# Reading each attention accumulator once, with two engines in turn, in a four-layer graph network

## The chip, the cores and the metric

The kernel runs on one core of one Trainium2 chip. The metric is the device time of one execution in microseconds (us), the median of several runs. All inputs lie in the chip's DRAM when it starts, and the result is written back there.

The core has a matrix engine (TensorE; in the profile PE for its matmuls and PEld for its weight loads), a vector engine (VectorE, DVE), a scalar engine for functions such as exp (ScalarE, ACT), a general engine (GpSimd, POOL) and an engine whose queue here only issues transfers (SyncE, SP). Each engine takes the instructions of its own queue in order; an instruction that waits holds up all that stand behind it on its engine. Matmul results go to PSUM[...]; all else lies in SBUF, 128 partitions wide.

## The reference

Four layers work on 4096 nodes with 256 features and one 4096 x 4096 adjacency matrix of zeros and ones. Each layer normalises its input, applies relu, runs a graph layer, and adds the result to the input:

```
h = max(layernorm(x), 0);  x = x + layer(h, adj)
layer 0: Wh = h @ W
         e  = leaky(Wh @ a_src + (Wh @ a_dst).T, 0.2), masked by adj
         h_attn = softmax(e, axis=1) @ Wh
         (then a dense part: several gated projections of Wh and h_attn)
layer 1: (adj == 1) @ h / degree @ W.T + b
layer 2: h2 = h @ W
         e  = leaky(h2 @ a[:256] + (h2 @ a[256:]).T, 0.01), masked by adj
         elu(softmax(e, axis=1) @ h2)
layer 3: softmax((h @ Wq) @ (h @ Wk).T, masked) @ (h @ Wv)
```

elu(z) is z where z is positive and exp(z) - 1 elsewhere. The change concerns the end of the attention in layers 0 and 2: the product of weights and values is divided by the sum of the weights, and in layer 2 elu is applied and the layer's input added.

## The kernel before

The state xs (128 x 32 x 256, float32) holds all 4096 rows in SBUF throughout, as 32 row tiles of 128 rows. Layers 0 and 2 share the class `Attention` (L160 to L314). It works on 8 blocks of four row tiles (RB = 4). For a block, the 4096 columns are gone through in 16 pairs of column tiles. The work on a pair is:

- `reach` (L216): DVE takes a running minimum over the mask codes of a later block (L229), which gives each row's largest logit. At the end of a block the minimum is transposed on TensorE (L238), reduced on DVE (L241 to L246), transposed back (L248), and sent through DRAM so that every partition has it as a row (L251, L253). `reach` runs 19 pairs ahead of the logits in the text of the program.
- `logits` (L258): DVE makes the logits y of four row tiles and one column tile (L265, twice a pair), POOL subtracts the mask code (L269). There are 8 buffers for y.
- three pairs later (`lag`), ACT takes the exponential (L295, twice a pair), and TensorE multiplies the four row tiles by the values v, which have 257 columns, the last of them ones (L306). The four products of a block gather in four PSUM accumulators `acc` of 128 x 257. Layer 0 has four such buffers, layer 2 five.
- after a block's last pair (L310 to L314), for each of its four row tiles: DVE takes the reciprocal of column 256 (L313), and `finish` is called.

`finish0` (L328 to L330) is one ACT instruction per row tile: acc times the reciprocal, into xs. `finish2` (L737 to L744) is four per row tile: ACT reads acc for exp (L740) and once more for relu (L742), then DVE adds min(exp, 1) and xs (L743), and relu and -1 (L744). The first product of the next block that needs an accumulator in use can start only when all reads of it are done.

In layer 0 the adjacency is read as it comes and transposed on TensorE (L348), turned into codes by ACT (L352) and stored; in layer 2 the codes come from DRAM (`stored`, L748 to L752) in pieces of 1 MB, four to a block, issued by SP (L751) into 7 buffers. A buffer is free again when POOL has subtracted the last pair of its piece.

The text of the program doesn't fix the order of the instructions on an engine. The framework that builds the program (Tile) lays them out by their dependencies and its own estimate of when each can run, and adds the waits; the order on the chip is then fixed. In the trace, running minima (L229) of later blocks stand between the steps of the block that ends.

PSUM, y and `turned` buffers are given out in the same way. Layer 3's preparation (L812 to L835) starts from xs right after layer 2, with its first tiles in the SBUF space that layer 2 leaves.

Of the kernel before, what the change touches and what calls it, by code (L numbers as in the profile page):

```python
# [11 lines left out]
F32 = mybir.dt.float32  # L12
# [3 lines left out]
AF = mybir.ActivationFunctionType  # L16
ALU = mybir.AluOpType
# [4 lines left out]
P = 128  # L22
# [19 lines left out]
def kernel(ctx: ExitStack, tc: tile.TileContext, w: dict, out: bass.AP):  # L42
    nc = tc.nc
    x, adj = w["x"], w["adj"]
    N, D = x.shape
# [8 lines left out]
    RB = 4  # L54
# [5 lines left out]
    const = ctx.enter_context(tc.tile_pool(name="const", bufs=1))  # L60
# [7 lines left out]
    ones = const.tile([P, P], F32, name="ones")  # L68
# [5 lines left out]
    xs = state.tile([P, NT, D], F32, name="xs")  # L74
# [49 lines left out]
    def preln(small, xb, h):  # L124

        mv = small.tile([P, BT, 2], F32, tag="pl_mv", name="pl_mv")
        for i in range(BT):
            stats_of(small, xb[:, i, :], mv[:, i, :], "pl")
        rs = rstd_of(small, mv, BT, "pl")
        off = small.tile([P, BT], F32, tag="pl_off", name="pl_off")  # L130
        nc.vector.scalar_tensor_tensor(off, mv[:, :, 0], -1.0, rs, ALU.mult, ALU.mult)
        for i in range(BT):
            nc.scalar.activation(
                h[:, i, :], xb[:, i, :], AF.Relu, scale=rs[:, i : i + 1], bias=off[:, i : i + 1]
            )
        return mv
# [23 lines left out]
    class Attention:  # L160
# [110 lines left out]
        def run(self, es, lead, n_acc, ahead=lambda n: None):  # L271

            self.y_p = es.enter_context(tc.tile_pool(name=f"{self.tag}_y", bufs=self.n_y))
            self.ps_b = es.enter_context(
                tc.tile_pool(name=f"{self.tag}_b", bufs=1, space=PSUM)
            )
            ps_acc = es.enter_context(
                tc.tile_pool(name=f"{self.tag}_acc", bufs=n_acc, space=PSUM)
            )
            pairs = [(b, c) for b in range(NRB) for c in range(0, NT, 2)]  # L280
            LAG = self.lag
            ys, accs = {}, {}
            for n in range(len(pairs) + LAG):
                if n < len(pairs):
                    b, c = pairs[n]
                    ahead(n)
                    if n + PPB + lead < len(pairs):
                        self.reach(n + PPB + lead)
                    ys[n] = y = self.y_p.tile([P, RB, 2, P], F32, tag="y", name="y")
                    self.logits(y, b, c, self.turned(b, c // QT))  # L290
                if n >= LAG:
                    b, c = pairs[n - LAG]
                    y = ys.pop(n - LAG)
                    for k in range(2):
                        nc.scalar.activation(  # L295
                            y[:, :, k, :], y[:, :, k, :], AF.Exp,
                            bias=self.sdst[:, c + k : c + k + 1],
                        )
                    if c == 0:
                        accs[b] = [  # L300
                            ps_acc.tile([P, D + 1], F32, tag="acc", name="acc")
                            for _ in range(RB)
                        ]
                    for k in range(2):
                        for r in range(RB):
                            nc.tensor.matmul(  # L306
                                out=accs[b][r], lhsT=y[:, r, k, :], rhs=self.v[:, c + k, :],
                                start=(c + k == 0), stop=(c + k == NT - 1),
                            )
                    if c == NT - 2:  # L310
                        for r, acc in enumerate(accs.pop(b)):
                            rden = self.small.tile([P, 1], F32, tag="rden", name="rden")
                            nc.vector.reciprocal(rden, acc[:, D : D + 1])  # L313
                            self.finish(b * RB + r, acc, rden)  # L314


    LEAD = 3
# [1 line left out]
    with ExitStack() as l0:  # L319
# [5 lines left out]
        bcw = w_early.tile([P, KD, 2 * S + 1], F32, name="bcw")  # L325
        bcb = w_early.tile([P, 2 * S + 1], F32, name="bcb")
        with ExitStack() as es:
            def finish0(t, acc, rden):  # L328

                nc.scalar.mul(xs[:, t, :], acc[:, 0:D], rden)  # L330

            turned = {}
            att = Attention(l0, es, "l0", 0.2, 3, 8, lambda b, q: turned[b, q], finish0)
# [23 lines left out]
            def ahead(n):  # L357
                if n + UPB + FRESH < NRB * UPB:
                    fresh(n + UPB + FRESH)
                if n % RB == 0:  # L360
                    b, q = n // UPB, n % UPB // RB
                    nc.sync.dma_start(out=codesT[b][q], in_=turned[b, q])
# [371 lines left out]
    with ExitStack() as es:  # L734
        work2 = es.enter_context(tc.tile_pool(name="l2_work", bufs=2))

        def finish2(t, acc, rden):  # L737

            e = work2.tile([P, D], F32, tag="e", name="e")
            nc.scalar.activation(e, acc[:, 0:D], AF.Exp, scale=rden)  # L740
            hp = work2.tile([P, D], F32, tag="hp", name="hp")
            nc.scalar.activation(hp, acc[:, 0:D], AF.Relu, scale=rden)  # L742
            nc.vector.scalar_tensor_tensor(e, e, 1.0, xs[:, t, :], ALU.min, ALU.add)  # L743
            nc.vector.scalar_tensor_tensor(xs[:, t, :], hp, -1.0, e, ALU.add, ALU.add)  # L744

        loaded = {}

        def stored(b, q):  # L748
            if (b, q) not in loaded:
                loaded[b, q] = turned_p.tile([P, RB, QT, P], BF16, tag="turned", name="turned")  # L750
                nc.sync.dma_start(out=loaded[b, q], in_=codesT[b][q])  # L751
            return loaded[b, q]  # L752

        att = Attention(es, es, "l2", 0.01, 3, 8, stored, finish2)
        turned_p = es.enter_context(tc.tile_pool(name="l2_turned", bufs=7))
        with ExitStack() as ps_:
            wp = ps_.enter_context(tc.tile_pool(name="l2_w", bufs=1))
            work = ps_.enter_context(tc.tile_pool(name="l2_prep", bufs=2))
            small = ps_.enter_context(tc.tile_pool(name="l2_s", bufs=4))
            pst = ps_.enter_context(tc.tile_pool(name="l2_pst", bufs=3, space=PSUM))  # L760
            psm = ps_.enter_context(tc.tile_pool(name="l2_psm", bufs=3, space=PSUM))
            att.weights(wp, work, w["L2_gnn_W"], (w["L2_gnn_a"],))

            def block2(b):
                h = work.tile([P, BT, D], F32, tag="h", name="h")
                preln(small, xs[:, ts(b, BT), :], h)
                yield
                hT = transposed_block(work, pst, h, "hT")
                yield
                att.project(b, hT, psm)  # L770
                yield
                for n in range(2 * b, 2 * b + 2 if b < NB - 1 else PPB + LEAD):
                    att.reach(n)

            run_staggered([block2(b) for b in range(NB)], 2)

        att.run(es, LEAD, 5)
# [233 lines left out]
```

## Time and profile before

| | |
|---|---|
| median of 3 runs | 3105.68 us (3105.03 to 3110.4) |
| profiled execution, its own time | 3108.19 us |
| span of its trace | 3106.4 us |
| TensorE matmul busy | 2881.5 us (93%) |
| DVE / ACT / POOL busy | 1847.5 / 1282.5 / 870.1 us |
| attention of layer 0 | about 111 to 632 us of the span |
| attention of layer 2 | about 1638 to 2135 us |
| granted TensorE clock, mean | 0.972 of full speed |

The table is read with the stages in mind: busy shares of the whole span mix stages with different limits. In the two attention stages TensorE does the same products, and what the other engines do shows only where TensorE stands still. A group of the profile's page has the line, engine, operation and tiles, the count, then the busy time and the mean length in ns, then the idle time of the engine just before these instructions and what ended most of it. A wait for several things is put down to the one that came last. Durations of the instructions concerned, from the trace (minimum / median / maximum in ns): L330 453/462/479, L740 452/473/498, L742 458/468/507, L743 415/420/1209, L744 415/420/2161, L313 141/168/170.

### The profile page before, as it was taken

Reading aid. Unit: us, or ns where it says so; the run is one execution under the profiler, and the core shown is the slowest. Engines: PE = TensorE matmul, PEld = TensorE weight load, DVE = VectorE, ACT = ScalarE, POOL = GpSimd, SP = SyncE. Lnnn points to the kernel's source line nnn. Section 1 sums busy time; section 2 is a strip of 40 time slices with the busy share of each in tenths; the row PEclk is TensorE's granted clock in tenths of the full one; section 3 lists DMA queues with packets and bytes.
Section 4 is the critical chain, followed back from the end, with each engine's and each line's share of the span. In section 5 each row is a group of like instructions: output and inputs, shape, how many; then the busy total and the mean of one; then the engine's idle time right before and its main releaser. Section 6 shows DMA issues by size and latency. Waiting matters only on the chain.

```text
span 3106.4 us, 34931 instructions
## 1 busy us (share of the span) xinstructions
PE 2881.5 (93%) x13344; PEld 2343.0 (75%) x13344; DVE 1847.5 (59%) x3322; ACT 1282.5 (41%) x1980; POOL 870.1 (28%) x604
## 2 busy tenths in 40 slices
PE   5799999979999999699968999899999999999999
PEld 4688888845555565588857887788888888888888
DVE  5767667324444444544479877755866656656653
ACT  5556655368888884400044443444111211211211
POOL 3556665533232332100016555562000000000000
PEclk9899999989999999899989999999999999999999
DMA  8666664054444441234222221202111111111100
GB/s 209 143 130 137 132 132 106 7 186 129 130 128 127 124 135 37 87 118 140 95 103 80 85 78 69 75 8 68 57 38 33 60 38 33 60 38 33 60 8 7
DMA packets 103128, 268.75 MB, mean 87 GB/s; under 512 B 10704, under 2 KB 24272, under 8 KB 94768
## 3 DMA queue, kind: packets, MB, share of 16 engines
q1 hardware_dynamic: 79104, 220.30, 21.3%
q0 software_dynamic: 22464, 45.51, 8.6%
q8 instruction: 104, 1.70, 0.2%
q10 hardware_dynamic: 1392, 0.72, 0.1%
q14 instruction: 64, 0.52, 0.1%
HBM read 262.22 MB, written 37.81 MB: 97 GB/s over the span
## 4 chain that ended last, share of the span: by engine, by line
PE 34%; issue 28%; ACT 11%; DMA 10%; DVE 10%; POOL 6%; POOLq 0%; ACTq 0%; SPq 0%; DVEq 0%
PE acc L306 16%; PE acc L717 8%; DMA a<-in_adj_dram 6%; PE mm L150 5%; ACT sign L507 5%; POOL y L269 4%; DVE run L229 3%; PE s L150 3%; DVE y L265 2%; PE acc L943 2%; DMA turned<-codesT 1%; DMA ab_row<-l_ab_d 1%; ACT zT L492 1%; ACT t L481 1%; ACT y L295 1%
## 5 line engine op out<-in xcount | busy, mean ns | idle before, releaser
L306 PE MATMUL acc<-v,y 128*128 128x257 f32 x4096 | 930.1, 386 | 52.9 <-ACT hp L742 27.8
L306 PEld LDWEIGHTS acc<-v,y 128*128 128x128 f32 x4096 | 777.2, 192 | 168.3 <-ACT hp L742 32.2
L269 POOL TENSOR_TENSOR y<-y,turned 128x1024 f32<-128x1024 f32 x256 | 544.0, 2137 | 323.1 <-DVE y L265 272.6
L295 ACT ACTIVATE y<-y,sdst 128x512 f32<-128x512 f32 x512 | 343.1, 715 | 359.7 <-POOL y L269 359.7
L265 DVE SCALAR_TENSOR_TENSOR y<-ab_row,cdst,b 128x512 f32<-128x512 f32 x512 | 361.4, 742 | 175.8 <-PE acc L306 110.1
L943 PE MATMUL acc<-v,y 128*128 128x257 f32 x2048 | 454.5, 380 | 0.4 <-DVE rden L951 0.4
L150 PE MATMUL s<-qT,hT 128*128 128x256 f32 x2048 | 445.2, 379 | 0.7 <-ACT qT L891 0.7
L150 PEld LDWEIGHTS s<-qT,hT 128*128 128x128 f32 x2048 | 389.0, 190 | 54.2 <-ACT qT L891 1.4
L943 PEld LDWEIGHTS acc<-v,y 128*128 128x128 f32 x2048 | 387.1, 190 | 55.9 <-issue 0.8
L936 ACT ACTIVATE y<-y 128x1024 f32<-128x1024 f32 x128 | 132.2, 1055 | 714.3 <-DVE y L935 710.0
L229 DVE SCALAR_TENSOR_TENSOR run<-turned,sd,run 128x512 f32<-128x512 bf16 x496 | 373.2, 752 | 68.1 <-DMA turned<-codesT 45.4
L507 ACT ACTIVATE sign<-a,limits 128x1024 bf16<-128x1024 int32 x256 | 294.0, 1148 | 85.4 <-DMA a<-in_adj_dram 81.2
L956 POOL DMA_DIRECT2D out_dram<-o x32 | 17.4, 542 | 934.9 <-DVE rden L951 932.0
L717 PE MATMUL acc<-v,eq 128*128 128x512 f32 x1024 | 240.3, 396 | 0.0
L905 DVE SCALAR_TENSOR_TENSOR y<-code,s 128x512 f32<-128x512 bf16 x256 | 175.8, 687 | 100.9 <-PE s L150 100.6
L717 PEld LDWEIGHTS acc<-v,eq 128*128 128x128 f32 x1024 | 191.9, 188 | 46.6 <-DVE eq L713 0.3
L935 DVE TENSOR_TENSOR y<-y,top 128x1024 f32<-128x1024 f32 x128 | 146.2, 1214 | 43.0 <-PE top L929 43.0
L912 DVE TENSOR_TENSOR mx<-mx,y 128x512 f32<-128x512 f32 x224 | 154.8, 691 | 7.5
L352 ACT ACTIVATE turned<-cT,log_wide 128x1024 bf16<-128x1024 bf16 x128 | 141.6, 1106 | 33.6 <-PE cT L348 33.3
L713 DVE TENSOR_SCALAR eq<-code 128x4096 fp32r<-128x4096 bf16 x32 | 73.4, 2294 | 115.8 <-PE acc L717 115.8
L150 PE MATMUL mm<-hsT,w_L_gnn_W_hz 128*128 128x512 f32 x256 | 118.3, 601 | 1.7 <-DVE hsT L570 1.7
L348 PE MATMUL cT<-identb,adj_t 128*128 128x128 bf16 x1024 | 83.2, 226 | 36.6 <-DVE identb L67 18.6
(219 smaller groups left out, 2742.8 us busy)
## 6 DMA issues: line engine op xcount, KB each, us to landing
a<-in_adj_dram SPq DMA_DIRECT2D x128, 512.0 KB, 3.7
adj_t<-in_adj_dram POOLq DMA_DIRECT2D x128, 256.0 KB, 4.5
codesT<-turned SPq DMA_DIRECT2D x32, 1024.0 KB, 5.2
code<-codesT SPq DMA_DIRECT2D x128, 256.0 KB, 3.8
turned<-codesT SPq DMA_DIRECT2D x32, 1024.0 KB, 4.9
code<-codesT SPq DMA_DIRECT2D x64, 512.0 KB, 4.8
ab_row<-l_ab_d SPq DMA_DIRECT2D x16, 512.0 KB, 3.8
xs<-in_x_dram SPq DMA_DIRECT2D x8, 512.0 KB, 12.2
```

What stands on the lines that cost most here:

```text
L150: nc.tensor.matmul(out=ps, lhsT=lhsT_of(k), rhs=rhs_of(k), start=(k == 0), stop=(k == n - 1))
L229: nc.vector.scalar_tensor_tensor(st["run"], code, self.sd[:, j, 1:2], st["run"], ALU.subtract, ALU.min)
L265: nc.vector.scalar_tensor_tensor(y[:, :, k, :], st["ab"][:, 0, :, :], self.cdst[:, c + k : c + k + 1], st["b"], ALU.add, ALU.max,)
L269: nc.gpsimd.tensor_tensor(y, y, mask[:, :, c % QT : c % QT + 2, :], ALU.subtract)
L295: nc.scalar.activation(y[:, :, k, :], y[:, :, k, :], AF.Exp, bias=self.sdst[:, c + k : c + k + 1],)
L306: nc.tensor.matmul(out=accs[b][r], lhsT=y[:, r, k, :], rhs=self.v[:, c + k, :], start=(c + k == 0), stop=(c + k == NT - 1),)
L507: nc.scalar.activation(sign, a, AF.Sign, bias=limits[:, v : v + 1], accum_out=over[:, t, v, q : q + 1],)
L717: nc.tensor.matmul(out=acc, lhsT=eq[:, ts(c, P)], rhs=v1[:, c, :, :], start=(c == 0), stop=(c == NT - 1),)
L905: nc.vector.scalar_tensor_tensor(y[:, :, c : c + 2, :], st["code"][:, :, c : c + 2, :], -BIG / UNIT, ps, ALU.mult, ALU.add,)
L912: nc.vector.tensor_tensor(mx, mx, y[:, :, c : c + 2, :], ALU.max)
L935: nc.vector.tensor_tensor(part, part, top, ALU.subtract)
L943: nc.tensor.matmul(out=accs[r], lhsT=st["y"][:, r, c, :], rhs=v3[:, c, :], start=(c == 0), stop=(c == NT - 1),)
```

## The change

`run` takes the four reciprocals of a block into one tile and calls `finish` once a block. In both layers ACT reads row tiles 0 and 2, DVE row tiles 1 and 3. In layer 2 the one read gives h = z - 1 in SBUF, and elu is then made from h for the four row tiles at once: exp(h + 1) on ACT, min(exp, 1) + xs on DVE, and max(h, -1) plus that on DVE. The work tiles of layer 2 are four times as wide (2 tags, 2 buffers each). A constant tile of -1 is new.

```diff
                     if c == NT - 2:
-                        for r, acc in enumerate(accs.pop(b)):
-                            rden = self.small.tile([P, 1], F32, tag="rden", name="rden")
-                            nc.vector.reciprocal(rden, acc[:, D : D + 1])
-                            self.finish(b * RB + r, acc, rden)
+                        done = accs.pop(b)
+                        rden = self.small.tile([P, RB], F32, tag="rden", name="rden")
+                        for r, acc in enumerate(done):
+                            nc.vector.reciprocal(rden[:, r : r + 1], acc[:, D : D + 1])
+                        self.finish(b, done, rden)
...
-            def finish0(t, acc, rden):
-                nc.scalar.mul(xs[:, t, :], acc[:, 0:D], rden)
+            def finish0(b, accs, rden):
+                for r, acc in enumerate(accs):
+                    dst, by = xs[:, b * RB + r, :], rden[:, r : r + 1]
+                    if r % 2:
+                        nc.vector.tensor_scalar(dst, acc[:, 0:D], by, None, ALU.mult)
+                    else:
+                        nc.scalar.mul(dst, acc[:, 0:D], by)
...
-        def finish2(t, acc, rden):
-            e = work2.tile([P, D], F32, tag="e", name="e")
-            nc.scalar.activation(e, acc[:, 0:D], AF.Exp, scale=rden)
-            hp = work2.tile([P, D], F32, tag="hp", name="hp")
-            nc.scalar.activation(hp, acc[:, 0:D], AF.Relu, scale=rden)
-            nc.vector.scalar_tensor_tensor(e, e, 1.0, xs[:, t, :], ALU.min, ALU.add)
-            nc.vector.scalar_tensor_tensor(xs[:, t, :], hp, -1.0, e, ALU.add, ALU.add)
+        minus = const.tile([P, 1], F32, name="minus")
+        nc.gpsimd.memset(minus, -1.0)
+        def finish2(b, accs, rden):
+            h = work2.tile([P, RB, D], F32, tag="hp", name="hp")
+            for r, acc in enumerate(accs):
+                by = rden[:, r : r + 1]
+                if r % 2:
+                    nc.vector.tensor_scalar(h[:, r, :], acc[:, 0:D], by, -1.0, ALU.mult, ALU.add)
+                else:
+                    nc.scalar.activation(
+                        h[:, r, :], acc[:, 0:D], AF.Identity, scale=by, bias=minus
+                    )
+            e = work2.tile([P, RB, D], F32, tag="e", name="e")
+            nc.scalar.activation(e, h, AF.Exp, bias=ones[:, 0:1])
+            rows = xs[:, ts(b, RB), :]
+            nc.vector.scalar_tensor_tensor(e, e, 1.0, rows, ALU.min, ALU.add)
+            nc.vector.scalar_tensor_tensor(rows, h, -1.0, e, ALU.max, ALU.add)
```

## The prediction

> **What bounds the kernel now.** I read the page first, then the busy table of the two attention stages, the list of waits of TensorE in each, and last the timeline around block ends. The page's groups show where TensorE's lost time is put down:
>
> ```profile
> L306 PE MATMUL acc<-v,y 128*128 128x257 f32 x4096 | 930.1, 386 | 52.9 <-ACT hp L742 27.8
> L306 PEld LDWEIGHTS acc<-v,y 128*128 128x128 f32 x4096 | 777.2, 192 | 168.3 <-ACT hp L742 32.2
> ```
>
> The columns after the bars are busy time, mean ns of one, and idle time before with its main releaser. Of the 52.9 us that the accumulating matmuls waited, 27.8 are put down to the last read of an accumulator in layer 2. The busy table of layer 0's attention (182 to 634 us) and layer 2's (1638 to 2135 us); the columns are length, then PE, PEld, DVE, ACT, POOL busy with counts, granted clock, DMA:
>
> ```profile
> 182.00:634.00 452.00, 439.34 (x2507) 378.78 (x2508) 276.23 (x444) 246.39 (x348) 266.37 (x185) 1.00 0.47 104
> 1638.00:2135.00 497.00, 467.06 (x2102) 401.61 (x2103) 371.69 (x641) 208.64 (x351) 276.64 (x134) 0.97 0.18 64
> ```
>
> TensorE is busy 97% and 94% of the time: 12.7 and 29.9 us idle are all that either stage can give, of 3106.4. The waits of TensorE by stage (total us, times, longest), layer 0 first:
>
> ```profile
> PE acc L306 <- ACT xs L330: 4.8, 6, 1.1
> ```
>
> ```profile
> PE acc L306 <- ACT hp L742: 27.8, 9, 6.1
> ```
>
> So at most 4.8 us hang on the reads in layer 0, and 27.8 in layer 2. But what makes the read late? The end of one block of layer 2, in the timeline (start, length, engine, line, and in brackets the idle time before it):
>
> ```profile
> 2006.82 0.32 SPq L751 DMA_DIRECT2D turned<-codesT  x1
> ...
> 2011.63 1.55 DVE L229 SCALAR_TENSOR_TENSOR run<-turned,sd,run 128x512 f32<-128x512 bf16 x2 [5.47 <-DMA turned<-codesT]
> 2013.08 1.40 DVE L265 SCALAR_TENSOR_TENSOR y<-ab_row,cdst,b 128x512 f32<-128x512 f32 x2
> 2014.40 0.75 DVE L229 SCALAR_TENSOR_TENSOR run<-turned,sd,run 128x512 f32<-128x512 bf16 x1
> ...
> 2015.06 0.23 DVE L313 RECIPROCAL rden<-acc 128x1 f32<-128x1 f32 x2
> ...
> 2015.26 0.47 ACT L740 ACTIVATE e<-acc,rden 128x256 f32<-128x256 f32 x1 [2.93 <-DVE rden L313]
> 2015.63 0.46 ACT L742 ACTIVATE hp<-acc,rden 128x256 f32<-128x256 f32 x1
> ...
> 2016.15 4.22 PE L306 MATMUL acc<-v,y 128*128 128x257 f32 x9 [5.16 <-ACT hp L742]
> ```
>
> Read it from the bottom. TensorE stood 5.16 us for the second of two ACT reads. ACT itself was idle for the reciprocal; the reciprocal stood in DVE's queue behind five instructions (L229, L265), and the first of those waited 5.47 us for a mask transfer issued at 2006.82. **The wait that carries the name of the ACT read is mostly a DMA wait on DVE**: of 5.16 us only 2016.15 - 2015.26 = 0.9 us are the two reads. The ends at 1825, 1889 and 1953 us look the same (4.16, 6.12, 4.70 us), the one at 1762 costs 2.50, the last nearly nothing. The end at 1702 is another kind (4.14 us): the first read stands in ACT's queue behind exponentials that wait for POOL.
>
> An end of a block in layer 0:
>
> ```profile
> 314.85 0.82 ACT L330 ACTIVATE xs<-acc,rden 128x256 f32<-128x256 f32 x2
> ...
> 316.16 0.72 ACT L295 ACTIVATE y<-y,sdst 128x512 f32<-128x512 f32 x1 [0.49 <-POOL y L269]
> 316.79 0.82 ACT L330 ACTIVATE xs<-acc,rden 128x256 f32<-128x256 f32 x2
> ...
> 317.29 2.87 PE L306 MATMUL acc<-v,y 128*128 128x257 f32 x12 [0.69 <-ACT xs L330]
> ```
>
> Two reads of four stand behind an exponential that waits for POOL; TensorE loses 0.69 us.
>
> **What the Trainium skill says.** "SBUF — State Buffer", Who interferes with whom: a DVE instruction with two SBUF inputs and a GpSimd one that reads SBUF exclude each other for the whole instruction. The trace agrees: L744 takes 0.42 us as a rule and 1.25 us where POOL works, ending 0.29 us after POOL does:
>
> ```profile
> 1957.00 2.48 POOL L269 TENSOR_TENSOR y<-y,turned 128x1024 f32<-128x1024 f32 x1 [3.31 <-DVE y L265]
> ```
>
> ```profile
> 1958.52 1.25 DVE L744 SCALAR_TENSOR_TENSOR xs<-hp,e 128x256 f32<-128x256 f32 x1
> ```
>
> "ScalarE: Activation LUTs", Table sets: identity is in every set. The trace agrees: L481 uses it among Silu and Exp and has no table load of its own. "VectorE: DVE Perf Modes", The TRN2 errata: a fixed cost per instruction, so few long ones are cheaper. The trace agrees: 128x256 takes 420 ns (L743), 128x1024 takes 1225 ns (L643), not 1680.
>
> **The change, part by part.** All sums are made against the profiled execution: span 3106.4, its own time 3108.19, which is 2.5 us above the median 3105.68 of the three runs; I take the differences over to the median.
>
> *Layer 0, reads on two engines.* ACT keeps 2 of 4 reads (462 ns each, L330) and gives 2 to DVE: 2 x 417 ns (the nearest row, L725, also 128x256 from PSUM) = 0.83 us a block. DVE is busy 276 of 452 us there, so this lies beside TensorE. Behind the new DVE reads stand logits (L265): POOL and then ACT get them 0.8 us later, once a block; covered, because TensorE has not once waited for an exponential after the start of the stage; without that cover it is 0.8 us x 7. What TensorE can get back is 4.8 us. The third accumulator's read stays on ACT and can still stand behind the exponential, so I take three quarters, **-3.6**; ends -4.8, and +3.5 if a DVE read lands behind two logits (1.39 us) and TensorE loses 0.5 us at each of 7 ends.
>
> *Layer 2, one read for two.* Before: two ACT reads an accumulator, 473 + 474 ns. After: one. The form (identity with a scale and a bias from SBUF) has no row from PSUM. Bounds: below, the 463 ns of L330; above, the 593 ns of L133, which has both operands but reads SBUF. "ScalarE: Activation LUTs", What ACT_TABLE_LOAD costs, puts 93 ns on each such operand; my estimate is 473 + 93 = 0.56 us. The first accumulator comes free 0.95 - 0.56 = 0.39 us sooner, at the 6 ends where TensorE waits long: -2.3. The later accumulators are read by DVE at the same time as ACT, so the small waits that follow the first at an end (27.8 less the six long ones, 26.8, is 1.0) go too: **-3.3** in all; ends -2.1 (593 ns and nothing more) and -3.9. The wait of DVE for the mask stays where it is: it is ahead of the reciprocals, and nothing in the edit touches the mask transfers, their buffers or the queue that issues them. What is late next is therefore what was late before.
>
> *Layer 2, elu from SBUF.* Removed: 8 STT of 420 ns = 3.4 us a block on DVE. Added there: 2 reads of 417 and 2 STT of 1225 = 3.3 us. Added on ACT: one exponential of 128x1024, 1.04 us by L642, 1.13 with its bias operand; ACT as a whole goes from 8 x 0.47 = 3.8 to 2 x 0.56 + 1.13 = 2.3 us. All this comes after the accumulators are free, so only later logits and exponentials see it: taken at nothing, with TensorE's prepared tiles as cover. The long STT have two SBUF inputs and exclude POOL: now L743 and L744 lose 34.6 - 64 x 0.42 = 7.7 us to it in all, 1 us a block; two meetings of up to 2.1 us replace eight, so -1 to +3 us a block on DVE, not on the path.
>
> *Added wait.* DVE's first STT now waits for a chain: all four reads, then the exponential on ACT. Behind it on DVE stand logits and running minima, and POOL waits for those. This is the third case below.
>
> *The end of layer 2.* Its last finish has nothing beside it. Last accumulator at 2131.45, reciprocal 0.17, DVE read 0.42, exponential 1.13, two STT 2.45: 2135.7, against 2134.74 before. The first copies into hT follow at 2135.31 now; some DVE work can go ahead of the STT, so I take **+0.5**, ends 0 and +1. The extra memset is one small POOL instruction, with 32 bytes of a constant: nothing. The work tiles grow by 12 KB a partition: a shift of later tiles, nothing if they fit.
>
> **Sum:** -3.6 - 3.3 + 0.5 = -6.4: 3101.8 for the profiled execution, **3099** for the median. Its own range with all the ends is 3105.7 - 8.7 = 3097 to 3105.7 + 2.4 = 3108. A measurement of this kernel can tell about 0.2%, 6.2 us, from no change.
>
> **The rivals.**
> *The order shifts to the good.* The order on each engine is made anew by the program's builder. If the reciprocals come ahead of the mask wait at the four ends that show it, up to 4.16 + 6.12 + 4.70 + 5.16 = 20.1 us less; as the mask still comes late and holds up the next logits, I take three quarters, 15: 3084. For it: only the order, not the data, puts them behind. Against: the mask's instructions were ahead at four ends running.
>
> *DVE stuck on the exponential, slower.* At 1702 us DVE waited 4.63 us for L740, because ACT had exponentials of later tiles ahead of it that waited for POOL, and POOL for DVE (4.64 us idle). The new exponential comes later in ACT's queue than the old one. If this recurs at the other six ends, DVE stands 6 x 4.6 = 28 us; where half reaches TensorE through logits, POOL and mask transfer, +14 and no gain in layer 2: 3105.7 - 3.6 + 0.5 + 14 = 3117. It decides from the point where the exponential ends more than the three DVE instructions then queued (2.2 us) after the last read. For it: from 1953.06 to 2016.15 us the chain that ended last runs through POOL, mask and DVE, so what delays DVE delays the block. Against: at five of seven ends DVE hardly waited for L740 (5.8 us in two).
>
> *The change doesn't do what it says:* the reads stand behind the same waits, and layer 0 gives nothing: -3.3 + 0.5: 3103; this is the upper part of the first case.
>
> **How the numbers follow.** First case 0.50 (0.32 of it under 3099.5, 0.18 above), good order 0.22, stuck DVE 0.28 (0.26 slower by over 0.2%, 0.02 within). Faster 0.54, within 0.2% 0.20, slower 0.26. The range leaves out the lower part of the good order (below 3079) and the upper part of the stuck DVE (above 3118).
>
> **What would show it.** Layer 0: TensorE's waits for a read of xs fall from 4.8 us to about 1. Layer 2: the waits for the read of acc fall from 27.8 to about 24, and the block ends still show a DVE wait for the mask ahead of the reciprocals. If they fall to under 10, the second case holds; if DVE waits over 10 us in all for the new exponential and POOL for logits longer than 152.4 us, the third. A clear gain with the mask wait still ahead of the reciprocals would make my reading of layer 2 wrong.

## The result, and the profile after

The changed kernel takes 3093.64 us (median of 10 runs, 3085.67 to 3101.83), the kernel before 3107.45 us beside it (10 runs, 3105.03 to 3110.98). The ratio is 0.9955, with a 95% interval of 0.9944 to 0.9965: 13.8 us less, twice the 6.4 us that were forecast.

The profiled execution of after is 3085.67 us, 8 us below its own median, so its span (3083.9 us) must not be set against the 3106.4 us of before. By stages the two differ as follows (us). Layer 0's attention is taken from its first logits to the first reciprocal of its last block, layer 2's from its first product to its last reciprocal:

| | layer 0 attention | dense part, layer 1 prepared | layer 2 attention | last reciprocal of layer 2 to first product of layer 3 |
|---|---|---|---|---|
| before | 519.2 | 672.1 | 493.3 | 81.3 |
| after | 519.5 | 665.5 | 478.9 | 80.8 |

The dense part is not the edit's: it lies between 661 and 672 us in all the executions of this study, whatever was edited in them (664.2 and 664.6 us in two that are before but for one number in layer 2). The gain is layer 2's, 14.4 us. The page's groups of the accumulating products after (busy time, mean ns, idle time before and what ended most of it):

```profile
L306 PE MATMUL acc<-v,y 128*128 128x257 f32 x4096 | 927.1, 385 | 42.5 <-ACT y L295 19.9
L306 PEld LDWEIGHTS acc<-v,y 128*128 128x128 f32 x4096 | 774.4, 192 | 158.1 <-ACT hp L754 22.7
```

The name of the accumulator's reader is gone from the first line: the wait for the first exponentials of a stage (19.9) is now the largest. The busy table with the columns of the prediction's: layer 0's attention after, then layer 2's before and after, from its first product to the end of its last reciprocal:

```profile
182.00:634.00 452.00, 439.44 (x2507) 378.78 (x2507) 281.61 (x459) 240.68 (x331) 265.95 (x185) 1.00 0.47 104
```

```profile
1638.77:2132.22 493.45, 464.68 (x2089) 399.78 (x2089) 368.30 (x632) 206.08 (x345) 275.87 (x134) 0.97 0.18 63
```

```profile
1631.18:2110.31 479.13, 460.49 (x2087) 396.91 (x2088) 364.04 (x601) 199.09 (x307) 279.07 (x134) 0.98 0.19 65
```

Layer 0 is as before (439.34 us of TensorE in 452). In layer 2 TensorE is idle for 18.6 us, where before had 28.8, and busy for 460.5 us, where before had 464.7. The waits of layer 2 after (us, times, longest):

```profile
DVE run L229 <- DMA turned<-codesT: 28.3, 10, 3.9
PE acc L306 <- ACT hp L754: 17.9, 12, 4.3
...
DVE e L760 <- ACT e L758: 6.5, 3, 4.5
```

Before had 27.8 us (9 times) on the read, and 45.4 us (14 times) on the mask. The end of the same block that the prediction showed, the sixth, now in after:

```profile
1995.08 1.33 ACT L295 ACTIVATE y<-y,sdst 128x512 f32<-128x512 f32 x2 [0.75 <-POOL y L269]
1996.03 0.76 DVE L229 SCALAR_TENSOR_TENSOR run<-turned,sd,run 128x512 f32<-128x512 bf16 x1 [3.27 <-DMA turned<-codesT]
1996.69 0.16 DVE L314 RECIPROCAL rden<-acc 128x1 f32<-128x1 f32 x1
...
1996.89 0.56 ACT L754 ACTIVATE hp<-acc,minus,rden 128x256 f32<-128x256 f32 x1 [0.48 <-DVE rden L314]
1997.35 0.71 ACT L295 ACTIVATE y<-y,sdst 128x512 f32<-128x512 f32 x1
...
1997.50 0.70 PE L306 MATMUL acc<-v,y 128*128 128x257 f32 x2 [2.36 <-ACT hp L754]
...
1997.96 0.55 ACT L754 ACTIVATE hp<-acc,minus,rden 128x256 f32<-128x256 f32 x1
...
1998.57 1.79 PE L306 MATMUL acc<-v,y 128*128 128x257 f32 x7 [0.36 <-ACT hp L754]
```

DVE still waits for the mask ahead of the first reciprocal. But between the mask's landing and the reciprocal there is now one running minimum (0.66 us); before there were five instructions (from 2011.63 to 2015.06, 3.43 us). At ends 3 to 6 of before five instructions stand there, at ends 2 to 6 of after one. Here is TensorE's stall split at that point for ends 4 to 6, where TensorE is idle before the mask lands in both kernels (us; TensorE's idle time starts at the product's start less the bracket):

| end | kernel | idle until mask lands | mask to reciprocal | to ACT's read | read to product | stall |
|---|---|---|---|---|---|---|
| 4 | before | 1.60 | 3.43 | 0.20 | 0.89 | 6.12 |
| 4 | after | 1.48 | 0.66 | 0.20 | 0.61 | 2.95 |
| 5 | before | 0.18 | 3.43 | 0.20 | 0.89 | 4.70 |
| 5 | after | 0.37 | 0.67 | 0.19 | 0.62 | 1.85 |
| 6 | before | 0.64 | 3.43 | 0.20 | 0.89 | 5.16 |
| 6 | after | 0.89 | 0.66 | 0.20 | 0.61 | 2.36 |

End 3 falls from 4.16 to 2.04 us. End 2 has only one running minimum there in before too; it is the short one of before's five mask ends (2.50 us) and falls least (1.71). The first end, of another kind, stays (4.14, 4.32).

Of the 14.4 us, 10.2 are less idle time of TensorE; the waits for the reads give 9.9 of them (27.8 less 17.9). The other 4.2 are less busy time for the same products, at a mean granted clock of 0.98 where before had 0.97. The mean hides short stretches at half clock. This is the one at the sixth end of before, and the 55 us that follow it (columns as above):

```profile
2013.92:2020.73 6.81, 4.58 (x11) 3.66 (x12) 6.67 (x16) 4.45 (x10) 2.76 (x2) 0.50 0.00 1
2021.00:2076.00 55.00, 54.51 (x254) 46.95 (x252) 26.67 (x46) 22.79 (x37) 33.28 (x16) 1.00 0.03 10
```

Each of the first six ends of before has such a stretch, of 3.4 or 6.8 us, which begins during the stall or within 1.9 us of its end: 27 us in all. After has four, at ends 1, 3, 4 and 5: 17 us. At half clock a stretch should cost about half its length, an estimate of 13.6 us for before and 8.5 for after from these lengths; the difference, 5.1, is near the 4.2 us measured. So a long stall cost more in these runs than its idle time. Which stall brings a stretch is not shown: one of 2.04 us has it (end 3 of after), one of 2.36 us has not (end 6).

### The profile page after: what moved, and what is told of

It is laid out like the page before. It is cut to its first block, busy times and chain, and to the rows that moved or that the text cites. A ratio compares the mean times of both kernels' runs of the same rounds, so it can differ in the third digit from the quotient of the medians.

```text
span 3083.9 us, 34813 instructions
## 1 busy us (share of the span) xinstructions
PE 2869.8 (93%) x13344; PEld 2336.0 (76%) x13344; DVE 1851.4 (60%) x3306; ACT 1271.7 (41%) x1924; POOL 873.3 (28%) x605
## 4 chain that ended last, share of the span: by engine, by line
PE 27%; issue 25%; DVE 3%; POOL 2%; DMA 1%; ACT 1%; POOLq 0%; DVEq 0%; ACTq 0%
PE acc L306 12%; PE acc L723 8%; PE s L150 3%; PE mm L150 2%; PE acc L960 2%; DVE run L229 1%; POOL y L269 1%; DMA turned<-codesT 1%; DVE y L265 1%; POOL pl_rs L116 1%; POOL out_dram L973 1%; DVE pl_st L121 0%; ACT y L295 0%; DVE hT L109 0%; PE tp L144 0%
## 5 line engine op out<-in xcount | busy, mean ns | idle before, releaser
L306 PE MATMUL acc<-v,y 128*128 128x257 f32 x4096 | 927.1, 385 | 42.5 <-ACT y L295 19.9
L229 DVE SCALAR_TENSOR_TENSOR run<-turned,sd,run 128x512 f32<-128x512 bf16 x496 | 373.4, 753 | 49.8 <-DMA turned<-codesT 28.3
L354 PE MATMUL cT<-identb,adj_t 128*128 128x128 bf16 x1024 | 83.2, 226 | 36.4 <-DVE identb L67 18.5
```

The source lines that it names most:

```text
L229: nc.vector.scalar_tensor_tensor(st["run"], code, self.sd[:, j, 1:2], st["run"], ALU.subtract, ALU.min)
L306: nc.tensor.matmul(out=accs[b][r], lhsT=y[:, r, k, :], rhs=self.v[:, c + k, :], start=(c + k == 0), stop=(c + k == NT - 1),)
```

## Theories

**Queue order.** What fell is DVE work between the mask and the reciprocal; that the reads are fewer or shared gives little. **Rival: the reads.** The gain comes from the reads themselves: half as many, shared by two engines. A third was formed after a run that refuted the first as the whole cause. **Row chain.** ACT's queue holds the exponentials of six pairs ahead of the first read of an accumulator. They are paced by POOL (2.1 us a pair) and start when a block's running minimum has been transposed, sent through DRAM and read back as a row. So two chains end at the read, the mask with the reciprocal behind it on DVE, and the row with the exponentials on ACT. At ends 2 to 6 of after, ACT was idle for 0.08 to 0.48 us between its last exponential and that read; at ends 3 to 6 of before for 2.9 to 3.2 us. So in after the second chain ends just before the first.

## The experiments

| kernel | time, us | ratio to before, 95% | layer 2 attention, us | TensorE's wait for reads, us |
|---|---|---|---|---|
| layer 0 part alone | 3109.10 | 1.0016 (1.0006 to 1.0025) | 493.4 | 28.1 |
| layer 2 part alone | 3090.92 | 0.9955 (0.9943 to 0.9968) | 478.1 | 17.5 |
| after, layer 2's reads all on ACT | 3108.87 | 1.0011 (1.0004 to 1.0018) | 491.8 | 27.5 |
| before, 8 mask buffers | 3097.60 | 0.9976 (0.9966 to 0.9987) | 486.4 | 20.9 |
| before, LEAD 2 | 3111.51 | 1.0028 (1.0018 to 1.0039) | 505.7 | 27.6 |
| after, LEAD 2 | 3102.01 | 0.9996 (0.9988 to 1.0004) | 493.1 | 20.2 |
| after, 8 mask buffers | 3093.04 | 0.9965 (0.9953 to 0.9977) | 481.5 | 19.0 |
| after, layer 0's first two reads on ACT | 3091.91 | 0.9961 (0.9949 to 0.9973) | 480.4 | 17.1 |
| after, DVE reads first | 3095.49 | 0.9980 (0.9972 to 0.9989) | 482.8 | 20.8 |
| DVE first, 8 mask buffers | 3096.34 | 0.9981 (0.9975 to 0.9988) | 484.0 | 20.1 |
| after, LEAD 4, 8 mask buffers | 3083.63 | 0.9946 (0.9934 to 0.9959) | 472.9 | 10.2 |
| DVE first, LEAD 4, 9 mask buffers | 3080.60 | 0.9935 (0.9921 to 0.9949) | 476.1 | 11.2 |

In the rows with DVE first, the last column adds the waits put to the DVE reciprocal tile to those put to ACT's read. Times are compared by their ratios: before took 3105.78 us beside the first four kernels, 3102.82 beside the next four and 3101.92 beside the last four. The stage and the waits are of one execution each. Three kernels have layer 2 exactly as in after (after, layer 2 part alone, layer 0's first two reads on ACT), and their stage lies between 478.1 and 480.4 us; a difference of 2 us in one stage is therefore not told apart from chance.

### One part at a time

Layer 0's new end alone, with layer 2 reading as before:

```diff
+                        for r, acc in enumerate(done):
+                            nc.vector.reciprocal(rden[:, r : r + 1], acc[:, D : D + 1])
+                        self.finish(b, done, rden)
...
+                    if r % 2:
+                        nc.vector.tensor_scalar(dst, acc[:, 0:D], by, None, ALU.mult)
```

> Only layer 0 has the new end of a block (two reads on ACT, two on DVE); layer 2 keeps its two ACT reads and its elu per row tile, with its reciprocals in one tile, and its queue order at the block ends in the steady state is that of before. Both theories of layer 2 say that nothing is gained there. If layer 0's reads had given the predicted 3.6 us the time would be about 3104; if TensorE's wait simply moved from the fourth read to the third, as the changed kernel's trace shows (five waits of 0.67 to 0.69 us before and after), it is that of before within 2 us.

Layer 0's attention is 520.1 us (519.2 before). TensorE's wait for the reads there is unchanged, 4.7 us in 7 times (4.8 in 6 before). Layer 0 gives nothing; the time is even 0.16% above before's, by an interval that lies just clear of 1, and neither attention stage shows where. Layer 2's new end alone:

```diff
-                    if r % 2:
-                        nc.vector.tensor_scalar(dst, acc[:, 0:D], by, None, ALU.mult)
-                    else:
-                        nc.scalar.mul(dst, acc[:, 0:D], by)
+                    nc.scalar.mul(xs[:, b * RB + r, :], acc[:, 0:D], rden[:, r : r + 1])
```

> Only layer 2 has the new end of a block; layer 0 has its four ACT reads. The order of layer 2's instructions on every engine is that of the changed kernel. Layer 2 as the whole cause: 3107.45 - 13.8 = about 3094, and a layer 2 (from its first product to its last) of about 479 us against 492 before. If the 6.8 us that the dense stage is shorter in the changed kernel's profile belong to the change through layer 0, the time is only about 3100.

It has the whole gain: the same ratio as after, and the same stage within a microsecond.

### The reads without the new order

Layer 2 as in after, one read for each accumulator and elu from SBUF, but ACT makes all four reads:

```diff
-                if r % 2:
+                if False:
                     nc.vector.tensor_scalar(h[:, r, :], acc[:, 0:D], by, -1.0, ALU.mult, ALU.add)
```

> As the changed kernel, but in layer 2 ACT reads all four accumulators, each once. The queue order on DVE at the last three of the long block ends is then again that of before: two running minima, two logits and one running minimum stand between the mask wait and the first reciprocal, where the changed kernel has one running minimum. Theory A (the gain in layer 2 is the order behind the mask wait): TensorE waits for the read about 4 to 5.5 us at these ends, as before less 0.4, so that the time is about 3101 to 3105. Theory B (the gain is that an accumulator is read once, by 0.55 us in place of 0.95): about 2 to 2.7 us at each end as in the changed kernel, time about 3094 to 3096.

The gain is gone. The program's builder laid out ends 3 to 6 as it had in before. The sixth end of this kernel:

```profile
2009.81 1.55 DVE L229 SCALAR_TENSOR_TENSOR run<-turned,sd,run 128x512 f32<-128x512 bf16 x2 [5.57 <-DMA turned<-codesT]
2011.26 1.40 DVE L265 SCALAR_TENSOR_TENSOR y<-ab_row,cdst,b 128x512 f32<-128x512 f32 x2
2012.58 0.75 DVE L229 SCALAR_TENSOR_TENSOR run<-turned,sd,run 128x512 f32<-128x512 bf16 x1
...
2013.23 0.23 DVE L314 RECIPROCAL rden<-acc 128x1 f32<-128x1 f32 x2
...
2013.43 1.93 ACT L754 ACTIVATE hp<-acc,minus,rden 128x256 f32<-128x256 f32 x4 [3.02 <-DVE rden L314]
...
2014.05 10.22 PE L306 MATMUL acc<-v,y 128*128 128x257 f32 x39 [4.37 <-ACT hp L754]
```

The five instructions are back, with their 3.42 us; from the first read's start to the product it is 0.62 us, as in after (before 0.89). Ends 3 to 6 stall for 4.06, 4.90, 5.83 and 4.37 us, while end 2, which has one running minimum there as in before and after, stalls for 2.21 us. So one read for two is worth 0.27 us at an end. The stage shows none of it: TensorE is idle for 29.6 us in it (28.8 before), and the 1.5 us that it is shorter (493.3 to 491.8) are busy time and within chance. What the reads don't give goes with the order.

### The mask alone

Before, with one more buffer for the mask pieces:

```diff
-        turned_p = es.enter_context(tc.tile_pool(name="l2_turned", bufs=7))
+        turned_p = es.enter_context(tc.tile_pool(name="l2_turned", bufs=8))
```

> The kernel before, with 8 buffers in place of 7 for layer 2's mask pieces, so that a piece can be fetched one piece (four pairs of column tiles, some 15 us) earlier. The reads, two on ACT for each accumulator, are as before. Theory A (TensorE's waits for the reads are DVE's wait for a mask): DVE's waits for masks fall from 45 us to under 20, TensorE's waits for the reads from 27.8 to under 15, the time to about 3090 to 3097. Theory B (the length of the reads): TensorE's waits stay at about 27 and the time at about 3106.

DVE's waits for the mask fall from 45.4 to 12.4 us, and half of the change's gain appears with none of its code: 6.9 us in the stage. TensorE's wait for the reads falls less than theory A said, to 20.9 us and not under 15. The same line in after:

> The changed kernel with 8 buffers for the mask pieces in place of 7. DVE's mask waits fall from 28 to about 10 us. In the kernel before this was worth 8.2 us; here the order already gives most of it, so 3 to 6 us less than the changed kernel, about 3088 to 3091.

Here nothing comes of it (478.9 to 481.5 us), though DVE's waits for the mask fall from 28.3 to 18.5. At ends 2 and 3 no mask wait stands ahead of the reciprocal any more, and ACT comes to the read only when its exponentials are through, 3.4 to 3.5 us after the reciprocal: the mask is not the only thing that ends late. But the order moved too. At end 4 two DVE instructions now stand between the mask's landing and the reciprocal, at end 5 four, where after has one. The fifth end:

```profile
1941.95 0.75 DVE L227 TENSOR_SCALAR run<-turned,sd 128x512 f32<-128x512 bf16 x1 [6.00 <-DMA turned<-codesT]
1942.61 1.40 DVE L265 SCALAR_TENSOR_TENSOR y<-ab_row,cdst,b 128x512 f32<-128x512 f32 x2
1943.93 0.75 DVE L229 SCALAR_TENSOR_TENSOR run<-turned,sd,run 128x512 f32<-128x512 bf16 x1
...
1944.59 0.16 DVE L314 RECIPROCAL rden<-acc 128x1 f32<-128x1 f32 x1
...
1945.40 1.23 PE L306 MATMUL acc<-v,y 128*128 128x257 f32 x2 [3.59 <-ACT hp L754]
```

It stalls for 3.59 us (1.85 in after), end 4 for 3.66 (2.95). So this run doesn't show what the buffer alone is worth in after.

Another way to bring the masks early is to ask for the running minima one pair later:

```diff
-                for n in range(2 * b, 2 * b + 2 if b < NB - 1 else PPB + LEAD):
+                for n in range(2 * b, 2 * b + 2 if b < NB - 1 else PPB + 2):
...
-        att.run(es, LEAD, 5)
+        att.run(es, 2, 5)
```

> The kernel before, with the running minimum of layer 2 going 2 pairs ahead of a block's end in place of 3. Reads and elu are those of before: two ACT reads for each accumulator. The built order changes: at six of the seven block ends 13 or 14 logits and no running minimum stand ahead of the reciprocals on DVE, so no mask is waited for there. Theory A (place in the queue): TensorE's waits for the reads fall from 27.8 us to under 12 and the time to about 3088 to 3097, by the order alone. Theory B (length of the reads): waits of 27 us and about 3106. A third outcome: the minimum comes 1 pair later to its transposes, so the next block's logits start later and TensorE waits for exponentials instead; then the waits for the reads fall and the time does not.

The mask waits fall to 11.1 us, as hoped, TensorE's waits for the reads stay (27.6 us), and the stage gets 12.4 us longer. Of these, 6.4 are waits of TensorE for DVE at the second transpose of the row (L248; 7.1 us, 0.7 in before), and 6.2 are busy time, at a granted clock of 0.96. The sixth end of this kernel:

```profile
2013.77 0.17 DVE L313 RECIPROCAL rden<-acc 128x1 f32<-128x1 f32 x1 [0.69 <-PE acc L306]
...
2013.82 1.34 ACT L295 ACTIVATE y<-y,sdst 128x512 f32<-128x512 f32 x2 [0.76 <-POOL y L269]
...
2015.90 1.34 ACT L295 ACTIVATE y<-y,sdst 128x512 f32<-128x512 f32 x2 [0.74 <-POOL y L269]
2017.99 0.72 ACT L295 ACTIVATE y<-y,sdst 128x512 f32<-128x512 f32 x1 [0.74 <-POOL y L269]
2018.62 0.46 ACT L740 ACTIVATE e<-acc,rden 128x256 f32<-128x256 f32 x1
...
2019.11 1.22 DVE L743 SCALAR_TENSOR_TENSOR e<-e,xs 128x256 f32<-128x256 f32 x1 [4.30 <-ACT e L740]
...
2019.49 2.94 PE L306 MATMUL acc<-v,y 128*128 128x257 f32 x6 [3.59 <-ACT hp L742]
```

The reciprocal is made at 2013.77 with no mask wait ahead of it, and the read starts 4.9 us later, behind exponentials that wait for POOL. The queue order as the whole cause is refuted by this run; the row chain was formed on it. DVE then waits for ACT's exponential of the accumulator, 31.3 us in 7 times: the mechanism of the prediction's third case, seen here and not in after. LEAD 2 in after:

> The changed kernel with the same 2 in place of 3 in layer 2. Again no running minimum stands in the two logits before the reciprocals. If the mask wait is what is left of TensorE's waits for the reads (17.9 us, of which some 2.2 us at five ends), they fall to under 8 us and the time from 3094 to about 3084 to 3088; if the lead is needed for the next block's rows, it is that of the changed kernel or worse.

The same loss: 14.2 us in the stage, which takes back the gain (ratio 0.9996). TensorE's waits for the reads are 20.2 us, not under 8.

### Layer 0's third read

After, with the halves of layer 0 in another order: ACT reads row tiles 0 and 1, DVE 2 and 3.

```diff
-                    if r % 2:
+                    if r > 1:
```

> The changed kernel with layer 0's accumulators shared out otherwise: ACT reads the first and the second, DVE the third and the fourth; layer 2 as in the changed kernel. In the changed kernel's trace ACT's second read (of the third accumulator) stands behind an exponential that waits for POOL, and TensorE waits 0.68 us for it at five ends. If that is why layer 0 gave nothing, the waits for reads of xs fall from 4.7 us to under 2 and the time by about 3 us, to 3090. If layer 0 is bound elsewhere (POOL, the rows sent through DRAM), the waits fall and the time stays.

TensorE's waits for reads in layer 0 fall from 4.7 to 2.0 us (2 times), and the stage stays at 519.5 us. Two of TensorE's waits in layer 0 (us, times, longest), in after and then in this kernel:

```profile
PE cT L354 <- ACT turned L358: 5.1, 8, 1.1
PE acc L306 <- ACT xs L336: 4.7, 7, 0.8
```

```profile
PE cT L354 <- ACT turned L358: 8.8, 14, 2.0
...
PE acc L306 <- ACT xs L336: 2.0, 2, 1.1
```

What the reads no longer cost is lost to the next wait, that of the transposes for ACT's codes. So a smaller stall at the reads gained nothing here.

### The row chain

The engines of layer 2's reads exchanged, so that DVE makes the first, with 7 and then with 8 mask buffers:

```diff
-                if r % 2:
+                if r % 2 == 0:
                     nc.vector.tensor_scalar(h[:, r, :], acc[:, 0:D], by, -1.0, ALU.mult, ALU.add)
```

> The kernel after with the engines of layer 2's reads exchanged: DVE reads accumulators 0 and 2, ACT 1 and 3 (layer 0 as it is). The first read no longer stands behind the twelve exponentials in ACT's queue; DVE's wait for the mask still stands ahead of the reciprocals. The mask alone (the theory that I held until the run with LEAD 2): nothing changes, TensorE's waits for the reads of an accumulator stay at 17 to 19 us and layer 2's attention at 479 us. Mask and row chain together (the theory since): the mask wait is still there and ends at about the same time as the exponentials, so again no gain: 16 to 19 us, stage 477 to 480 us. Only if the exponentials alone set the read, the waits fall to about 9 and the stage to 471 us.

> As the last, and with 8 mask buffers in place of 7: neither the mask wait nor the exponentials stand ahead of the first read. Mask alone: as the kernel after with 8 buffers, which gave nothing: waits of TensorE 17 to 19 us, layer 2's attention 479 to 482 us. Mask and row chain together: both covers are gone for the first time; a reciprocal and a DVE read of 0.48 us remain, about 0.9 us at each of six ends and 4.3 us at the first: waits of 8 to 11 us, stage 469 to 473 us, the time about 3085 us beside 3093.6 of the kernel after.

The first gains nothing, as both theories said, and is even 4 us worse in the stage than after (their ranges ended at 480 us and at 19 us of waits; it measured 482.8 and 20.8). Its time, too, is above after's beyond both intervals. The second misses what the row chain was taken to say: 20.1 us, not 8 to 11. One of its ends shows why:

```profile
1814.90 0.17 DVE L314 RECIPROCAL rden<-acc 128x1 f32<-128x1 f32 x1
1815.10 0.48 DVE L752 TENSOR_SCALAR hp<-acc,rden 128x256 f32<-128x256 f32 x1
1815.50 0.16 DVE L314 RECIPROCAL rden<-acc 128x1 f32<-128x1 f32 x1
1816.58 1.34 ACT L295 ACTIVATE y<-y,sdst 128x512 f32<-128x512 f32 x2 [0.75 <-POOL y L269]
...
1818.66 0.72 ACT L295 ACTIVATE y<-y,sdst 128x512 f32<-128x512 f32 x1 [0.28 <-POOL y L269]
...
1819.29 1.01 ACT L754 ACTIVATE hp<-acc,minus,rden 128x256 f32<-128x256 f32 x2
...
1819.89 4.41 PE L306 MATMUL acc<-v,y 128*128 128x257 f32 x19 [2.87 <-ACT hp L754]
```

The first accumulator is read by 1815.58. The second, whose reciprocal is done at 1815.66, is ACT's, and ACT starts it at 1819.29, when the exponentials ahead of it are through: TensorE stands for 2.87 us with no mask wait ahead of these two reciprocals. The exchange had moved the wait from the first accumulator to the second; my expectation had overlooked that. Nor was the mask gone: at ends 4 and 5 mask waits of 3.84 and 6.06 us still stand ahead of the first reciprocal, with two and four DVE instructions behind them, and these ends stall for 4.27 and 3.95 us. So the run didn't take both covers away, and tests the row chain less than it was meant to. That all four reads on DVE would get round it was not tried. The other way is to start the chain earlier, with LEAD 4 and ACT reading first as in after:

```diff
-        turned_p = es.enter_context(tc.tile_pool(name="l2_turned", bufs=7))
+        turned_p = es.enter_context(tc.tile_pool(name="l2_turned", bufs=8))
...
-        att.run(es, LEAD, 5)
+        att.run(es, 4, 5)
```

(the range of the preparation's `reach` likewise)

> The kernel after with LEAD 4 in place of 3 in layer 2 and 8 mask buffers: the row of a block is asked for one pair (about 3.8 us) earlier, reads as in the kernel after (ACT first). Mask alone: with 8 buffers and one pair more to hold, as the kernel after at best: waits of TensorE for the reads 17 to 20 us, stage 479 to 482 us. Mask and row chain together: the twelve exponentials end some 2 to 4 us earlier at a block's end, before the block's last product; the read waits only for its reciprocal: waits 8 to 12 us, stage 469 to 474 us.

For the reads this is what the row chain said. The waits of this kernel in layer 2:

```profile
PE acc L306 <- ACT hp L754: 10.2, 10, 2.9
DVE run L229 <- DMA turned<-codesT: 9.1, 4, 3.3
PE abT L248 <- DVE ab L246: 9.0, 7, 1.6
...
DVE run L227 <- DMA turned<-codesT: 6.9, 2, 5.3
```

The first end, which neither kernel of the change had moved, falls from 4.17 to 0.93 us, and the stage is 472.9 us, 8.6 less than with 8 buffers and LEAD 3. But the stage did not get there as the row chain says. TensorE now waits 9.0 us for DVE at the second transpose of the row (0.7 with LEAD 3), so its idle time falls by only 2.0 us, to 19.2; after, with 18.6, has no more. The other 6.7 us are busy time. The stage in this kernel, with the columns of the busy table:

```profile
1634.74:2107.78 473.04, 453.83 (x2087) 391.50 (x2088) 373.98 (x601) 197.94 (x307) 274.96 (x134) 1.00 0.18 63
```

The same products take 453.8 us at a granted clock of 1.00, where 8 buffers and LEAD 3 take 460.5 at 0.98: no stretch at half clock stands at a block end here. That the forecast for the stage was met is therefore luck in its mechanism; the forecast for the reads was not. Whether the clock stayed up because the stalls are shorter and more spread is not shown: the longest here is 2.91 us, and no run varied that alone. All three edits together, with 9 buffers:

> All three together, with 9 mask buffers: DVE reads accumulators 0 and 2 first, LEAD 4. Mask alone: nothing beyond the kernel after (479 us in layer 2, waits 17 us). Mask and row chain together: not below the better of the two kernels before it, since each of them already takes both away: waits 7 to 10 us, stage 468 to 472 us, time 3082 to 3086 us. If the stage stays at 475 us or above in all three, the row chain is wrong as well and the cause of the remaining stalls is open.

The stage misses its 468 to 472 us (476.1) and the waits their 7 to 10 (11.2), and with 484.0 us before it two of the three kernels lie above the 475 us at which, had all three done so, the row chain was to be given up. The time is the lowest of the study, 3080.60 us, and the ratio too. Layer 2's preparation is 6.4 us shorter in it (70.1 us, 76.5 in after), for a reason that was not tried. Both kernels with LEAD 4 beat before clear of their intervals (by 0.54% and 0.65%). Their intervals overlap with that of after (0.9955), so that they beat it too is likely and not shown.

## Why the prediction was right and wrong

**The direction and the range held** (3099 us forecast, 3079 to 3118; 3093.64 measured), but the range held by luck. The first case, on which the sum rests, gave itself 3097 to 3108 us and a gain of 8.7 at most; 13.8 came, between that case and the second (3084). The sum did not hold term by term: two of its three terms gave next to nothing, and what gave the gain stood in it at nothing.

*Layer 0, -3.6: nothing.* The profile of after shows the cause that the prediction had named for a loss of a quarter, the third accumulator's read. It stands behind an exponential that waits for POOL; an end in layer 0 after:

```profile
315.84 0.72 ACT L295 ACTIVATE y<-y,sdst 128x512 f32<-128x512 f32 x1 [0.83 <-POOL y L269]
...
316.47 0.46 ACT L336 ACTIVATE xs<-acc,rden 128x256 f32<-128x256 f32 x1
...
316.98 2.87 PE L306 MATMUL acc<-v,y 128*128 128x257 f32 x12 [0.68 <-ACT xs L336]
```

The stall is 0.68 us, before 0.69. TensorE's next product needs that accumulator, so sharing the other reads moves nothing. The step that failed is "I take three quarters": one late read out of four holds the whole stall. And the run with two early ACT reads showed that even the stall is covered, by the wait for codes.

*Layer 2, one read for two, -3.3: nothing that the stage shows.* The new read takes 0.55 us (forecast 0.56), and the first accumulator comes free 0.27 us sooner at an end rather than 0.39, 1.6 us at six ends. The small waits did not go, they grew: ACT's second read stands behind an exponential, and five ends have a second stall of 0.36 to 0.58 us, 2.4 in all, where before had one of 0.20. The one takes back the other.

*"The wait of DVE for the mask stays where it is."* It did, and that was not the point. **The step that failed is the reading of the stall: "mostly a DMA wait on DVE".** The prediction's own fence has the parts. TensorE went idle at 2010.99 (2016.15 - 5.16) and the mask landed at 2011.63: the mask is 0.64 us of the 5.16. The 5.47 us in DVE's bracket had mostly passed while TensorE still worked. The five instructions behind the mask are 3.43 us, and these depend on the order alone. The prediction held that only a reciprocal placed ahead of the mask wait would gain (its second case, 3084 us), and took its absence for no gain. What came is between the two: mask wait ahead, four of five instructions no longer between, 2.77 us at each of ends 4 to 6, and some 2 at end 3. That is a second case in its mechanism and two thirds of it in size (9.9 us of stall where 15 were named). The sign that the prediction set against itself, a clear gain with the mask wait still ahead, is just what was seen.

*"12.7 and 29.9 us idle are all that either stage can give."* Layer 2 had more to give. The 0.97 beside the 29.9 in the prediction's own table is the clock, and of the 14.4 us that the stage lost, 4.2 were busy time. No term of the sum stands for it.

*Elu from SBUF, taken at nothing: held.* DVE waits for the new exponential for 6.5 us in 3 times (5.8 before), so the third case did not occur. The two long instructions of elu on DVE (SCALAR_TENSOR_TENSOR, STT for short) do meet POOL's, and the block's critical part is over by then.

*The end of layer 2, +0.5: -0.5.* Last reciprocal to first product of layer 3 is 80.8 us, before 81.3.

What remains open: what brings the stretches at half clock, and why the builder laid the queue out so well with two DVE reads and so badly with none. The runs show that the order and the stall go together (end 2 against ends 3 to 6, of before and of the kernel with all reads on ACT); they don't show what in its estimates decides. The instructions' place was not set by hand in any run.

## What to carry to other kernels

When one engine stands for another, count from the moment it goes idle and split the stall along the chain: the idle bracket of the engine further back says how long that engine waited, not how much of it anyone felt. "Perfetto Trace Analysis", Optimization Strategy, in the Trainium skill says that a gap which repeats can mean too few buffers; here a mask buffer more was worth 6.9 us in one kernel and nothing in the other, where a second chain ended within 0.5 us of the first and the buffer changed the order as well. And where a builder orders the queues, an edit's first effect may be a new order: compare what stands between the last arrival and the instruction that the critical engine needs. Last, set idle time and busy time of a stage side by side before a gain is put down to a wait: in the kernel with LEAD 4 and 8 buffers the wait that was aimed at fell by 8.8 us, the idle time by 2.0, and the rest came with the clock.

## What the runs showed of the hardware

- DVE's read of a 128x256 accumulator with a scalar for each partition takes 476 ns (464 to 485) in layer 2; the sum of an accumulator and an SBUF tensor of that size (L725), which the prediction had taken for it, takes 417.
- ACT's read of an accumulator with scale and bias both from SBUF takes 552 ns, with the scale alone 462 (L330): 90 ns for the operand. "ScalarE: Activation LUTs", What ACT_TABLE_LOAD costs, has 93; the trace agrees.
- A 128x1024 STT of two SBUF tensors, 1.22 us alone, took 3.05 us at 1882 us of the kernel with DVE first and 8 buffers, where POOL's subtraction (2.12 us) was under way: the exclusion that the prediction quotes acts on the long form as it does on the short one.
- TensorE's granted clock in layer 2 falls to 0.50 for 3.4 or 6.8 us at a block end with a long stall, six times before, four times after, and not once with LEAD 4 and 8 buffers. The means are 0.97, 0.98 and 1.00, and TensorE's busy time for the same products 464.7, 460.5 and 453.8 us.
